# Tiles 4 to 7 as two units of two tiles instead of one of four, in a conditioned residual layer

## The chip, the cores and the metric

The kernel runs on one core of one Trainium2 chip. The metric is the device time of one execution in microseconds (us). Engines are called by the names that the profile uses: PE is the matrix engine (PEld its weight loads), DVE the vector engine, ACT the scalar engine, POOL the GpSimd engine, and SP the engine whose queue issues nearly all DMA transfers of this kernel.

## What is computed

```python
def _L0_cond_ref(hidden0, hidden1, x, W, b):     # x: (4, 1024, 512), W: (1536, 512)
    hidden = jnp.concatenate([hidden0, hidden1], axis=-1)         # both are cond_512: (4, 256)
    x_mean = jnp.mean(x, axis=1, keepdims=True)
    ones_L = jnp.ones((1, L, 1), dtype=x.dtype)
    fused = jnp.concatenate([x, x_mean * ones_L, hidden[:, None, :] * ones_L], axis=-1)
    return jax.nn.relu(jnp.einsum('bld,do->blo', fused, W) + b)
return x + _L0_cond_ref(cond_512, cond_512, x, L0_cond_W, L0_cond_b)
```

Each of the four batch rows has 1024 positions of 512 channels. Only the first third of W meets every position. The other two thirds meet the mean and the condition, which are the same for all positions of a row: they give one bias vector for each row.

## The kernel before

**Tiles and products.** The 4096 positions are 32 tiles of 128, eight to a batch row. A tile's product with the first third of W needs the tile transposed, with its 512 channels cut into J = 4 quarters of 128 (index j). Each float32 factor is split into a high and a low part (`w_hi`, `w_lo`; `his`, `los`), and each quarter takes three matmuls: hi by hi, lo by hi, hi by lo. `p5.2` is the triple of tile 5, quarter 2 (line 365); `p5.2.1` is one matmul of it. The 12 matmuls of a tile gather in one of five PSUM banks, `bank(t)` = `ps_o[t % 5]`.

**Units.** Tiles are transposed unit by unit (`UNITS`). Tiles 0 to 3 are units of one tile, transposed on PE from the plain copy of x. The others are units of four tiles. For these, four DMA transfers (`Zu.i`, 256 KB each) bring the tiles into one of three buffers `zs`, arranged so that DVE's transpose of 32x32 blocks finishes the job: `Tu.j` (line 258) transposes quarter j of all tiles of the unit, 128x512 elements, and needs all four transfers. `hu.j` (ACT, line 265) rounds it to `his` and adds up its columns into `sums`; `lu.j` (DVE or POOL, line 271) takes the remainder to `los`. Quarters 0 and 2 are turned into PSUM (`ps_x`), 1 and 3 into SBUF (`turned`): four slots, each of which is written again when the h and the l of its last content are done.

**Bias of a row.** When all sums of row r are in, `to` (POOL, lines 301 to 307) gives the mean. `as` (ACT, line 311) puts the condition's part (`ac`, `g`, `d`) into the bank `acc`; four `m` (DVE, line 316) add the mean times the second third of W, which the transfers `M0` to `M3` bring. Then `f` (ACT, line 324), `fa` (DVE, 328), `vh` (ACT, 332) and `vl` (DVE, 336) fold and split it, and `pb` (PE, line 340) spreads it over the partitions, from where `bc` (ACT) copies it to `biases`.

**The way out.** `K` (lines 436 and 438, from tile 12 on 446) empties a bank into a parking buffer, `b` and `r` add bias and apply relu, `F` adds x, and `S` stores the tile. F needs the plain copy of x, which `Xg.h` brings two tiles at a time.

**What sets the order.** Each engine runs its instructions in the order in which the names stand in `ORDER`, a list written out by hand or by a search; a letter behind @ names the engine where there is a choice (d DVE, a ACT, p POOL). An engine whose next instruction waits does nothing else. SP's transfers also go in this order, and at most eight are under way: each waits until the one eight before it has landed. PE's instructions around `pb0` stand in lines 33 and 34 of `ORDER`: eight triples of tiles 8 to 11, then `pb0`.

Of the kernel before, what the change touches and what calls it, by code (L numbers as in the profile page):

```python
# [25 lines left out]
h1.3 p1.0.1 Z4.1 p1.1.0 wh2@a l1.2@d p1.1.1 y2.0@d p0.2.0 wl2@p l1.3@d T2.0 T2.1 T2.2 T2.3 p1.2.0 Z4.3 p0.2.1 h2.0  # L26
h2.1 h2.2 h2.3 l2.0@d l2.1@d wh3@a C p1.2.1 p0.1.2 p1.1.2 l2.2@d l2.3@d wl3@d p2.0.0 p2.0.1 p0.2.2 V p0.3.0 B p1.3.0
y3.0@d p0.3.1 p1.3.1 T3.0 T3.1 T3.2 T3.3 p1.2.2 p0.3.2 h3.0 h3.1 p1.3.2 l3.0@d h3.2 l3.1@d p2.0.2 h3.3 l3.2@d l3.3@d
p2.1 p2.2 p2.3 p3.0 p3.1 Z5.0 Z5.2 Z5.1 p3.2 Z5.3 M1 M0 M2 Z6.0 M3 Z6.2 Z6.1 Z6.3 T4.0 T4.3 h4.0 T4.1 h4.3 l4.0@d h4.1
l4.3@p t3 p3.3 T4.2 Z7.0 Z7.2 Z7.1 Z7.3 K2@d l4.1@p K1@a p4.0 t2 h4.2 ac0@p p6.0 l4.2@d K0@a p4.3 t0 K3@d p5.3 t1  # L30
ac1@d g0.0 p7.2 p6.2 d0.0 g0.1 p5.2 d0.1 g1.0 p5.0 T5.1 T5.3 p5.1 d1.0 T5.2 p6.3 K5@a T5.0 Z8.0 Z8.2 X1.0 Z8.1 Z8.3
X1.1 as0 p4.2 to0 g1.1 p7.3 h5.1 m0.0 p6.1 g2.0 l5.1@p m0.1 p4.1 h5.2 m0.2 p7.1 K4@a m0.3 h5.3 p7.0 K6@a p8.1 l5.3@p
l5.2@d h5.0 p10.1 f0 d1.1 p9.1 fa0 p10.3 l5.0@d vh0 d2.0 p8.2 g2.1 vl0 p11.2 K7@a T6.3 d2.1 p11.3 T6.2 h6.3 p8.0 T6.0
# [1 line left out]
l6.2@d p12.3 r2@a m1.0 K9@a p8.3 F1@p S1 Z9.1 X3.0 Z9.3 T7.3 p11.0 T7.1 h7.3 p12.2 b0@p m1.1 h7.1 p12.0 T7.2 K8@a
p12.1 b3@p g3.0 T7.0 p11.1 K10@a m1.2 h7.2 d3.0 p13.1 m1.3 h7.0 p14.0 l7.0@d f1 b4@p p13.3 r0@a l7.2@d p14.1 r3@a T8.2
l7.3@p p15.0 fa1 p13.0 T8.0 vh1 F2@p S2 Z10.0 X2.1 Z10.2 p15.1 K11@a vl1 p13.2 F0@d S0 Z10.1 b6@p p15.2 T8.3 pb1
l7.1@p p14.3 bc1@a as2 p14.2 K13 F3@p r6@a p16.0 K12 h8.3 p15.3 K14 h8.2 l8.3@p T8.1 p17.0 b5@d h8.1 p19.3 b9@p h8.0
p17.3 r4@a l8.0@d p19.2 to2 g3.1 l8.2@d F4@p S4 Z10.3 X3.1 S3 p16.2 r5@a m2.0 p18.3 K15 b8@p p18.2 m2.1 p16.3 d3.1
m2.2 p19.0 m2.3 p18.1 F5@p S5 X5.0 T9.0 p16.1 f2 fa2 p20.3 b11@p T9.3 p17.2 vh2 h9.0 vl2 p17.1 F6@p S6 X4.0 X4.1 h9.3  # L40
T9.2 p19.1 l8.1@d b7@p p20.0 pb2 p18.0 bc2@a l9.3@p h9.2 p20.2 K17 r7@a p20.1 K16 as3 F7@p S7 X7.0 X6.1 X5.1 p22.2
T9.1 l9.0@d p21.3 h9.1 T10.0 r8@a p21.1 l9.1@p K19 r11@a p22.1 r9@a l9.2@d b10@p p22.0 r14@a K18 p21.2 r13@a T10.1
h10.0 p24.2 F13@p S13 T10.2 h10.1 p24.1 T10.3 h10.2 F8@p F9@d S9 S8 X6.0 p21.0 r15@a p24.0 r10@a F11@p S11 X7.1 K20
h10.3 p22.3 K21 r17@a p23.1 to3 r21@a p23.0 F10@p S10 m3.0 r18@a p23.3 r20@a m3.1 p26.1 l10.3@p m3.2 p25.0 K22 F21@p
S21 p23.2 m3.3 r22@a p26.2 F15@p S15 f3 p24.3 r12@a fa3 p27.3 F17@p S17 K23 vh3 p25.1 r16@a vl3 p25.2 r19@a F16@p S16
r23@a p26.0 l10.0@d p25.3 F19@p S19 pb3 p26.3 bc3@a F12@p S12 P28 p27.1 K25 p27.2 l10.2@d P30 F18@p p28.2 F14@d S14
S18 r25@a p30.2 l10.1@p K26 p28.0 F25@d S25 P31l p27.0 F23@p S23 r26@a p30.0 K24 p31.2l F26@p K27 p31.0l r24@a P29
p31.3l F20@p p30.3 p31.1l P31r F31l S31l S26 F22@d S22 S20 p29.1 p28.1 r27@d p29.0 F24@d S24 F27@p p28.3 p29.3 F28 S28
S27 p30.1 p29.2 F30 S30 p31.1r F29 S29 p31.0r p31.3r p31.2r F31r S31r
# [445 lines left out]
```

## Time and profile before

| | |
|---|---|
| time, median of 3 runs (lowest, highest) | 100.74 us (100.49, 102.19) |
| the profiled execution's own time | 101.55 us |
| its span, first to last instruction of the program | 99.8 us |
| busy in the span: PE, PEld | 95.2 us (95%), 76.3 us (76%) |
| busy in the span: POOL, DVE, ACT | 79.9 us (80%), 76.5 us (77%), 61.8 us (62%) |
| granted TensorE clock | 9 of 10 or more in all 40 slices of the span |

How to read it: the span leaves out 1.75 us that lie around the program in that execution. A busy share is an average over stages; whether an engine is waited for is told by the rows of that stage. Matmuls are pipelined, so the distance between two starts tells the pace, not the length of one row.

### The profile page before, as it was taken

To read this page: it belongs to the slowest core of one execution; us is meant where nothing else is said; L and a number is where in the kernel's file an instruction comes from. 1 tells how busy PE (TensorE), PEld (TensorE's weight loads), DVE (VectorE), ACT (ScalarE), POOL (GpSimd) and SP (SyncE) were. 2 spreads that over 40 slices of the span, in tenths; PEclk is the share of its full clock that TensorE was granted. 3 is DMA by queue.
4 is the path that set the end of the run, shared out by engine and by line. 5 is a ranking of instruction groups with operands and counts; after the bars stand their busy time and mean duration, and the time that the engine had idled before them with its cause. 6 is when DMAs were issued, how large, how long until landed. Compare 5 with 4: busy or idle time off the path is not lost.

```text
span 99.8 us, 1456 instructions
## 1 busy us (share of the span) xinstructions
PE 95.2 (95%) x426; PEld 76.3 (76%) x426; DVE 76.5 (77%) x131; ACT 61.8 (62%) x160; POOL 79.9 (80%) x77
## 2 busy tenths in 40 slices
...
GB/s 62 336 339 290 230 282 284 208 249 262 228 214 221 220 224 214 183 219 250 278 258 285 243 289 274 329 393 407 352 292 388 407 385 283 315 225 214 306 382 150
DMA packets 25361, 27.36 MB, mean 274 GB/s; under 512 B 1413, under 2 KB 16009, under 8 KB 25354
## 3 DMA queue, kind: packets, MB, share of 16 engines
...
q8 instruction: 3, 0.05, 0.2%
...
HBM read 18.88 MB, written 8.39 MB: 273 GB/s over the span
## 4 chain that ended last, share of the span: by engine, by line
PE 47%; DMA 35%; DVE 6%; SPq 6%; issue 1%; ACT 1%; DVEq 0%
PE po L365 46%; DMA x<-in_L_cond_W_dram 14%; DMA z<-in_x_dram 11%; DMA w_mean<-in_L_cond_W_dram 10%; SPq L145 6%; DVE lo L271 2%; DVE acc L328 1%; PE acc L340 1%; DVE acc L316 1%; DVE v_acc L336 1%; DVE o L236 1%; ACT fold L324 1%; ACT v_acc L332 1%; DVE w_hi L217 1%; DVE x L409 0%
## 5 line engine op out<-in xcount | busy, mean ns | idle before, releaser
L365 PE MATMUL po<-w_hi,hi 128*128 128x512 f32 (+1 forms) x133 | 50.6, 384 | 0.0
L365 PE MATMUL po<-w_hi,lo 128*128 128x512 f32 (+1 forms) x132 | 50.4, 384 | 0.0
L365 PE MATMUL po<-w_lo,hi 128*128 128x512 f32 (+1 forms) x132 | 50.1, 384 | 0.0
L460 POOL TENSOR_TENSOR x<-o,x 128x512 f32<-128x512 f32 x22 | 29.8, 1380 | 0.4 <-DVE o L451 0.4
L365 PEld LDWEIGHTS po<-w_hi,hi 128*128 128x128 f32 x133 | 24.9, 188 | 5.4 <-ACT o L438 0.6
L365 PEld LDWEIGHTS po<-w_hi,lo 128*128 128x128 f32 x132 | 24.8, 188 | 5.3 <-DVE lo L271 0.6
L365 PEld LDWEIGHTS po<-w_lo,hi 128*128 128x128 f32 x132 | 24.7, 188 | 4.9 <-POOL w_lo L221 0.2
L271 POOL TENSOR_TENSOR lo<-xT,hi 128x512 fp32r<-128x512 f32 x13 | 17.7, 1365 | 9.5 <-ACT hi L265 9.5
L453 ACT ACTIVATE o<-o 128x512 f32<-128x512 f32 x27 | 15.7, 621 | 3.3 <-DVE o L446 3.0
L442 POOL TENSOR_TENSOR o<-o,bias 128x512 f32<-128x512 f32 x10 | 13.8, 1390 | 0.0
L316 DVE SCALAR_TENSOR_TENSOR acc<-w_mean,tot,acc 128x512 f32<-128x512 f32 x16 | 12.0, 748 | 1.6 <-POOL tot L307 1.2
L265 ACT ACTIVATE hi<-px 128x512 fp32r<-128x512 f32 (+1 forms) x22 | 10.4, 477 | 4.1 <-DVE px L258 3.5
L446 DVE TENSOR_TENSOR o<-po,bias 128x512 f32<-128x512 f32 x16 | 10.5, 680 | 2.8 <-ACT bias L344 1.4
L258 DVE STREAM_TRANSPOSE px<-z 128x512 f32<-128x512 f32 x14 | 9.5, 699 | 3.7 <-DMA z<-in_x_dram 3.6
L271 DVE TENSOR_TENSOR lo<-px,hi 128x512 fp32r<-128x512 f32 (+1 forms) x22 | 11.6, 536 | 0.8 <-ACT hi L265 0.7
L258 DVE STREAM_TRANSPOSE xT<-z 128x512 f32<-128x512 f32 x14 | 9.4, 686 | 2.1 <-DMA z<-in_x_dram 2.1
L265 ACT ACTIVATE hi<-xT 128x512 fp32r<-128x512 f32 x14 | 8.8, 625 | 1.3 <-DVE xT L258 1.3
L293 ACT ACTIVATE term<-wc,cT 128x512 f32<-128x512 f32 x8 | 5.7, 716 | 2.3 <-DVE cT L279 1.6
L297 POOL TENSOR_TENSOR cond<-b_sb,term 128x512 f32<-128x512 f32 x4 | 5.2, 1300 | 1.0 <-ACT term L293 1.0
L438 ACT ACTIVATE o<-po 128x512 f32<-128x512 f32 x10 | 5.9, 586 | 0.1
L460 DVE TENSOR_TENSOR x<-o,x 128x512 f32<-128x512 f32 x6 | 5.6, 935 | 0.0
L297 POOL TENSOR_TENSOR cond<-cond,term 128x512 f32<-128x512 f32 x4 | 5.2, 1293 | 0.3 <-ACT term L293 0.2
...
## 6 DMA issues: line engine op xcount, KB each, us to landing
...
x<-in_L_cond_W_dram SPq DMA_DIRECT2D x1, 1024.0 KB, 10.0
...
```

The source lines that it names most:

```text
L145: (nc.scalar if e == "a" else nc.sync).dma_start(**kw)
L258: nc.vector.transpose(xT.rearrange("p (n q e) -> p n q e", q=Q // E, e=E), zs[z_of(u)][:, : n * NQ].rearrange("p n (q j e) -> p n j q e", ...
L265: nc.scalar.activation(his[buf][:, col : col + m], xT, AF.Copy, accum_out=sums[:, r, j, s : s + 1])
L271: nc_of[e].tensor_tensor(los[buf][:, col : col + m], xT, his[buf][:, col : col + m].bitcast(F32), ALU.subtract)
L297: nc.gpsimd.tensor_tensor(conds[r % 2], conds[r % 2] if k else b_sb, terms[k], ALU.add)
L316: nc.vector.scalar_tensor_tensor(acc, w_mean[:, j, :], tot[:, r, j : j + 1], acc, ALU.mult, ALU.add)
L365: nc.tensor.matmul(v, lhsT=a[:, col : col + P], rhs=m, start=WAYS[t] != "I" and key not in done, stop=done.count(key) == 3 * J - 1, skip_g ...
L438: nc.scalar.activation(o, bank(t), AF.Copy)
L442: nc_of[e].tensor_tensor(o, o, biases[r], ALU.add)
L446: nc.vector.tensor_tensor(o, bank(t), biases[r], ALU.add)
L453: nc.scalar.activation(o, o, AF.Relu)
L460: nc_of[e].tensor_tensor(x_tile(t), o, x_tile(t), ALU.add)
```

## The change

Tiles 4 to 7 become two units, (4, 2) and (6, 2). Unit 4 is tiles 4 and 5, unit 5 is tiles 6 and 7, and the later units are counted up by one: tiles 8 to 11 are unit 6 now, tiles 12 to 15 unit 7, and so on. Each of the two new units has its own four transfers of 128 KB into a half of the same buffer, and its own four T, h and l of 128x256 elements; so there are four transfers, T, h and l more. Row 0 has six units instead of five, and `to0` adds them in the same number of steps. The matmuls are the same ones. The middle of `ORDER` (the work between the first triples of tile 2 and `S1`) is written anew; behind it the old order goes on with the new unit numbers.

```diff
-l6.3@p T6.1 Z9.0 X2.0 Z9.2 pb0 p10.0 bc0@a h6.0 p10.2 b1@p h6.1 l6.0@d p9.3 h6.2 b2@d p9.0 as1 to1 p9.2 r1@a l6.1@p
...
+l6.2@d Z9.1 T7.3 d1.1 Z9.3 T7.1 T7.0 X1.0 p10.1 g2.1 d2.1 p9.3 T7.2 Z10.0 X2.0 Z10.2 p10.0 pb0 bc0@a b1@p h7.3 h7.1
...
-    UNITS = [(0, 1), (1, 1), (2, 1), (3, 1)] + [(t, 4) for t in range(4, NT, 4)]
+    UNITS = [(0, 1), (1, 1), (2, 1), (3, 1), (4, 2), (6, 2)] + [(t, 4) for t in range(8, NT, 4)]
...
-    sums = sb("sums", [P, B, J, 5])
+    sums = sb("sums", [P, B, J, 6])
     tot = sb("tot", [P, B, J])
-    pre = sb("pre", [P, J, 2])
+    pre = sb("pre", [P, J, 3])
...
     def z_of(u):
-        return (u - len(BY_PE)) % Z_BUFS
+        t0, n = UNITS[u]
+        return zs[(t0 // 4 - 1) % Z_BUFS][:, t0 % 4 * NQ : (t0 % 4 + n) * NQ]
...
-                dma(e, out=z[i * Q : (i + 1) * Q, : n * NQ], in_=zv[r, i, :, k0 * NQ : (k0 + n) * NQ, :])
+                dma(e, out=z[i * Q : (i + 1) * Q], in_=zv[r, i, :, k0 * NQ : (k0 + n) * NQ, :])
...
-                xT = (turned if j % 2 else ps_x)[j // 2]
+                xT = (turned if j % 2 else ps_x)[j // 2][:, :m]
...
-            if n == 5:
-                add(pre, v[:, :, :2], v[:, :, 2:4], ALU.add)
-                add(pre[:, :, 0], pre[:, :, 0], v[:, :, 4], ALU.add)
+            if n == 6:
+                add(pre, v[:, :, :3], v[:, :, 3:6], ALU.add)
+                add(pre[:, :, 0], pre[:, :, 0], pre[:, :, 2], ALU.add)
```

On PE, `pb0` now stands behind six triples of tiles 8 to 11 instead of eight. Three other places follow row by row.

**First place: DVE, tiles 4 to 7.** z_69 is the buffer of these tiles, px and xT the slots of a turned quarter, hi_78 belongs to tile 3, cT to the condition, o_105 and o_106 are banks being emptied (K2, K3). Before, from the first transpose of these tiles:

```order
L258 STREAM_TRANSPOSE px_140<-z_69 128x512
L258 STREAM_TRANSPOSE xT_121<-z_69 128x512
L258 STREAM_TRANSPOSE xT_120<-z_69 128x512
L271 TENSOR_TENSOR lo_93<-px_140,hi_79 128x512
L279 STREAM_TRANSPOSE cT<-bias_118 32x64
L258 STREAM_TRANSPOSE px_141<-z_69 128x512
L436 COPY o_105<-po_137 128x512
```

And now, from the same place; the first two transposes need the transfers of tiles 4 and 5 alone, the third those of tiles 6 and 7:

```order
L260 STREAM_TRANSPOSE xT_120<-z_69 128x256
L260 STREAM_TRANSPOSE xT_121<-z_69 128x256
L273 TENSOR_TENSOR lo_92<-acc,hi_78 128x128
L273 TENSOR_TENSOR lo_92<-po_139,hi_78 128x128
L273 TENSOR_TENSOR lo_92<-px_140,hi_78 128x128
L260 STREAM_TRANSPOSE xT_120<-z_69 128x256
L273 TENSOR_TENSOR lo_95<-xT_120,hi_81 128x256
L260 STREAM_TRANSPOSE px_140<-z_69 128x256
```

Two half transposes have moved ahead of tile 3's remainders, and a third ahead of tile 3's last remainder.

**Second place: DVE, from the transposes of tiles 8 to 11 to the end of row 0's bias.** z_70 is the buffer of these tiles, acc<-w_mean,tot,acc the four m0. Before:

```order
L258 STREAM_TRANSPOSE xT_120<-z_70 128x512
L258 STREAM_TRANSPOSE xT_121<-z_70 128x512
L258 STREAM_TRANSPOSE px_141<-z_70 128x512
L258 STREAM_TRANSPOSE px_140<-z_70 128x512
L316 SCALAR_TENSOR_TENSOR acc<-w_mean,tot,acc 128x512 x4
L271 TENSOR_TENSOR lo_99<-px_141,hi_85 128x512
L328 TENSOR_TENSOR acc<-acc,fold 64x512
L271 TENSOR_TENSOR lo_97<-px_140,hi_83 128x512
L336 TENSOR_TENSOR v_acc<-acc,v_acc 64x512
```

And now:

```order
L260 STREAM_TRANSPOSE xT_120<-z_70 128x512
L260 STREAM_TRANSPOSE xT_121<-z_70 128x512
L260 STREAM_TRANSPOSE px_141<-z_70 128x512
L319 SCALAR_TENSOR_TENSOR acc<-w_mean,tot,acc 128x512
L260 STREAM_TRANSPOSE px_140<-z_70 128x512
L439 COPY o_106<-po_138 128x512
L319 SCALAR_TENSOR_TENSOR acc<-w_mean,tot,acc 128x512 x3
L273 TENSOR_TENSOR lo_97<-px_140,hi_83 128x512
L331 TENSOR_TENSOR acc<-acc,fold 64x512
L339 TENSOR_TENSOR v_acc<-acc,v_acc 64x512
```

The first m0 stands before the last transpose, a bank's copy (K3) has come into the chain between the m0, and one remainder (l6.2) now stands behind v_acc.

**Third place: SP's transfers.** z_69 is here the buffer of tiles 16 to 19, z_70 of tiles 20 to 23, z_71 of tiles 24 to 27; x_66 is the plain copy of tiles 4 to 7. Before:

```order
L145 DMA z_69<-in_x_dram 32x16x128 x4
L145 DMA z_70<-in_x_dram 32x16x128 x2
L145 DMA x_66<-in_x_dram 128x2x512
L145 DMA z_70<-in_x_dram 32x16x128 x2
L145 DMA x_66<-in_x_dram 128x2x512
L145 DMA z_71<-in_x_dram 32x16x128
```

And now:

```order
L146 DMA z_69<-in_x_dram 32x16x128 x4
L146 DMA z_70<-in_x_dram 32x16x128 x4
L146 DMA x_66<-in_x_dram 128x2x512
L146 DMA z_71<-in_x_dram 32x16x128
L146 DMA x_67<-in_x_dram 128x2x512
```

The first half of x_66 has moved behind the last two transfers of tiles 20 to 23; its second half goes eight rows further back, behind the transfers of tiles 24 to 27. Further ahead, the four w_mean transfers now stand together; before, the fourth stood behind the first transfer of tiles 12 to 15.

## Rows read from the trace of the kernel before

**Rows 1.** The profile's page: the span and each engine's busy time.

```profile
span 99.8 us, 1456 instructions
PE 95.2 (95%) x426; PEld 76.3 (76%) x426; DVE 76.5 (77%) x131; ACT 61.8 (62%) x160; POOL 79.9 (80%) x77
```

**Rows 2.** The chain of waits in order of time: start us, us, what.

```profile
20.38 9.48 DMA w_mean<-in_L_cond_W_dram
...
35.61 10.99 DMA z<-in_x_dram
...
48.78 0.70 DVE v_acc L336
...
50.02 13.62 PE po L365 x60
```

**Rows 3.** The timeline of PE at 18 us: start us, us, engine line operation out<-in.

```profile
17.71 0.39 PE L365 MATMUL po<-w_hi,hi 128*128 128x512 f32 x1
18.11 0.50 PE L365 MATMUL po<-w_hi,lo 128*128 128x512 f32 x1
...
18.80 0.50 PE L365 MATMUL po<-w_hi,hi 128*128 128x512 f32 x1
19.13 0.40 PE L365 MATMUL po<-w_hi,lo 128*128 128x512 f32 x1
```

**Rows 4.** The timeline of DVE, tiles 4 to 7; in brackets idle time before, and releaser.

```profile
15.58 0.73 DVE L258 STREAM_TRANSPOSE px<-z 128x512 f32<-128x512 f32 x1 [2.23 <-DMA z<-in_x_dram]
...
17.41 0.65 DVE L271 TENSOR_TENSOR lo<-px,hi 128x512 fp32r<-128x512 f32 x1
```

**Rows 5.** The timeline of ACT, the copy of bank 1 (K1).

```profile
18.16 0.58 ACT L438 ACTIVATE o<-po 128x512 f32<-128x512 f32 x1
```

**Rows 6.** The timeline of PE at 49 us, the second row's bias (L340).

```profile
48.89 0.39 PE L365 MATMUL po<-w_lo,hi 128*128 128x512 f32 x1
49.52 0.50 PE L340 MATMUL acc<-v_acc,ones 128*128 128x512 f32 x1 [0.24 <-DVE v_acc L336]
49.86 0.39 PE L365 MATMUL po<-w_hi,hi 128*128 128x512 f32 x1
```

**Rows 7.** The timeline of PE, the first row's bias (pb0).

```profile
34.61 0.39 PE L340 MATMUL acc<-v_acc,ones 128*128 128x512 f32 x1
```

**Rows 8.** The timeline of DVE, tiles 8 to 11 and the first row's bias.

```profile
24.42 1.31 DVE L258 STREAM_TRANSPOSE xT<-z 128x512 f32<-128x512 f32 x2 [2.10 <-DMA z<-in_x_dram]
25.65 1.28 DVE L258 STREAM_TRANSPOSE px<-z 128x512 f32<-128x512 f32 x2
27.49 3.22 DVE L316 SCALAR_TENSOR_TENSOR acc<-w_mean,tot,acc 128x512 f32<-128x512 f32 x4 [0.56 <-POOL tot L307]
...
32.73 0.68 DVE L336 TENSOR_TENSOR v_acc<-acc,v_acc 64x512 fp32r<-64x512 f32 x1
```

**Rows 9.** The timeline of POOL, the same stretch.

```profile
25.12 1.30 POOL L297 TENSOR_TENSOR cond<-b_sb,term 128x512 f32<-128x512 f32 x1
...
27.23 0.22 POOL L307 TENSOR_SCALAR tot<-tot 128x4 f32<-128x4 f32 x1
...
29.41 1.29 POOL L271 TENSOR_TENSOR lo<-xT,hi 128x512 fp32r<-128x512 f32 x1 [0.70 <-ACT hi L265]
```

**Rows 10.** Groups by line and shape: line engine op shapes xcount | busy us, mean ns | idle.

```profile
L271 DVE TENSOR_TENSOR lo<-px,hi 128x128 fp32r<-128x128 f32 x8 | 2.2, 284 | 0.0
...
L436 DVE COPY o<-po 128x512 f32<-128x512 f32 x2 | 1.3, 667 | 0.0
...
L409 DVE SCALAR_TENSOR_TENSOR x<-po,x 128x256 f32<-128x256 f32 x2 | 0.8, 424 | 2.3 <-PE po L365 2.3
```

**Rows 11.** Stretches: us, busy us (instructions) of PE, PEld, DVE, ACT, POOL; PEclk, DMA share, GB/s.

```profile
40.00:45.00 5.00, 5.00 (x23) 4.14 (x23) 4.69 (x8) 4.96 (x13) 5.00 (x5) 1.00 1.15 201
...
65.00:70.00 5.00, 5.00 (x24) 4.14 (x23) 4.90 (x9) 4.65 (x11) 5.00 (x5) 1.00 1.04 400
```

**Rows 12.** The timeline of POOL, the residual add of tile 4 (F4).

```profile
56.10 1.29 POOL L460 TENSOR_TENSOR x<-o,x 128x512 f32<-128x512 f32 x1
```

More of the change, by code (lines that the diff above doesn't have):

```diff
@@ L25 @@
 T1.0 T1.1 T1.2 T1.3 wh1@d h1.0 p0.0.2 l1.0@d h1.1 p0.1.0 p1.0.0 Z4.2 h1.2 p0.1.1 l0.2@d l0.3@d wl1@p p1.0.2 l1.1@d
[L26 to L33, printed above, removed]
-l6.3@p T6.1 Z9.0 X2.0 Z9.2 pb0 p10.0 bc0@a h6.0 p10.2 b1@p h6.1 l6.0@d p9.3 h6.2 b2@d p9.0 as1 to1 p9.2 r1@a l6.1@p
@@ L35 @@
[L35 to L49, printed above, removed]
+h1.3 p1.0.1 Z4.1 p1.1.0 wh2@a l1.2@d p1.1.1 y2.0@d p0.2.0 wl2@p l1.3@d T2.0 T2.1 T2.2 T2.3 p1.2.0 Z4.3 Z5.0 Z5.2 Z5.1
@@ new lines @@
+Z5.3 p0.2.1 h2.0 h2.1 h2.2 h2.3 l2.0@d l2.1@d wh3@a C p1.2.1 p0.1.2 p1.1.2 l2.2@d p2.2 l2.3@d wl3@d p2.0.0 p2.0.1
+p0.2.2 V p0.3.0 B p1.3.0 y3.0@d p0.3.1 p1.3.1 T3.0 T3.1 T4.1 T3.2 T3.3 p1.2.2 p0.3.2 h3.0 p2.1 h3.1 K0@a T4.3 p1.3.2
+l3.0@d p3.0 h3.2 l3.1@d p3.1 l3.2@d h4.1 l4.1@p p5.1 T5.1 h5.1 l5.1@d T4.0 h4.3 Z6.3 l4.3@p p4.1 t3 t2 p3.2 p2.0.2
+h3.3 l3.3@d t1 t0 T4.2 p5.3 p3.3 ac0@p Z6.1 K1@a h4.0 Z6.0 p2.3 h4.2 T5.3 l4.2@d T5.2 p4.2 ac1@d p4.3 g0.0 l4.0@d p4.0
+T5.0 g0.1 h5.2 K2@d p5.2 h5.0 l5.2@d p6.2 d0.0 d0.1 h5.3 l5.3@p to0 p5.0 Z6.2 as0 M0 l5.0@d T6.1 g1.0 d1.0 p6.1 K4@a
@@ new lines @@
+T6.3 g1.1 M1 T6.2 h6.1 K5@a p6.0 l6.1@p p6.3 K6@a p7.2 g2.0 M3 h6.3 p7.1 m0.0 T6.0 h6.0 K3@d p7.3 p7.0 l6.3@p p9.1
+m0.1 M2 m0.2 m0.3 Z7.2 K7@a Z7.3 Z7.0 Z7.1 f0 l6.0@d fa0 h6.2 vh0 p8.1 p10.3 Z8.0 Z8.3 Z8.2 vl0 Z8.1 Z9.0 Z9.2 d2.0
+l6.2@d Z9.1 T7.3 d1.1 Z9.3 T7.1 T7.0 X1.0 p10.1 g2.1 d2.1 p9.3 T7.2 Z10.0 X2.0 Z10.2 p10.0 pb0 bc0@a b1@p h7.3 h7.1
+h7.0 p11.3 p10.2 l7.0@d h7.2 b2@d p9.0 l7.3@p as1 to1 p9.2 r1@a l7.1@p l7.2@d p8.0 p11.2 p12.3 p8.2 r2@a m1.0 K9@a
+p8.3 F1@p S1 Z10.1 X3.0 Z10.3 T8.3 p11.0 T8.1 h8.3 p12.2 b0@p m1.1 h8.1 p12.0 T8.2 K8@a p12.1 b3@p g3.0 T8.0 p11.1
@@ new lines @@
+K10@a m1.2 X1.1 h8.2 d3.0 p13.1 m1.3 h8.0 p14.0 l8.0@d f1 b4@p p13.3 r0@a l8.2@d p14.1 r3@a T9.2 l8.3@p p15.0 fa1
+p13.0 T9.0 vh1 F2@p S2 Z11.0 X2.1 Z11.2 p15.1 K11@a vl1 p13.2 F0@d S0 Z11.1 b6@p p15.2 T9.3 pb1 l8.1@p p14.3 bc1@a as2
+p14.2 K13 F3@p r6@a p16.0 K12 h9.3 p15.3 K14 h9.2 l9.3@p T9.1 p17.0 b5@d h9.1 p19.3 b9@p h9.0 p17.3 r4@a l9.0@d p19.2
+to2 g3.1 l9.2@d F4@p S4 Z11.3 X3.1 S3 p16.2 r5@a m2.0 p18.3 K15 b8@p p18.2 m2.1 p16.3 d3.1 m2.2 p19.0 m2.3 p18.1 F5@p
+S5 X5.0 T10.0 p16.1 f2 fa2 p20.3 b11@p T10.3 p17.2 vh2 h10.0 vl2 p17.1 F6@p S6 X4.0 X4.1 h10.3 T10.2 p19.1 l9.1@d b7@p
@@ new lines @@
+p20.0 pb2 p18.0 bc2@a l10.3@p h10.2 p20.2 K17 r7@a p20.1 K16 as3 F7@p S7 X7.0 X6.1 X5.1 p22.2 T10.1 l10.0@d p21.3
+h10.1 T11.0 r8@a p21.1 l10.1@p K19 r11@a p22.1 r9@a l10.2@d b10@p p22.0 r14@a K18 p21.2 r13@a T11.1 h11.0 p24.2 F13@p
+S13 T11.2 h11.1 p24.1 T11.3 h11.2 F8@p F9@d S9 S8 X6.0 p21.0 r15@a p24.0 r10@a F11@p S11 X7.1 K20 h11.3 p22.3 K21
+r17@a p23.1 to3 r21@a p23.0 F10@p S10 m3.0 r18@a p23.3 r20@a m3.1 p26.1 l11.3@p m3.2 p25.0 K22 F21@p S21 p23.2 m3.3
+r22@a p26.2 F15@p S15 f3 p24.3 r12@a fa3 p27.3 F17@p S17 K23 vh3 p25.1 r16@a vl3 p25.2 r19@a F16@p S16 r23@a p26.0
@@ L50 @@
+l11.0@d p25.3 F19@p S19 pb3 p26.3 bc3@a F12@p S12 P28 p27.1 K25 p27.2 l11.2@d P30 F18@p p28.2 F14@d S14 S18 r25@a
+p30.2 l11.1@p K26 p28.0 F25@d S25 P31l p27.0 F23@p S23 r26@a p30.0 K24 p31.2l F26@p K27 p31.0l r24@a P29 p31.3l F20@p
+p30.3 p31.1l P31r F31l S31l S26 F22@d S22 S20 p29.1 p28.1 r27@d p29.0 F24@d S24 F27@p p28.3 p29.3 F28 S28 S27 p30.1
+p29.2 F30 S30 p31.1r F29 S29 p31.0r p31.3r p31.2r F31r S31r
 """.split()
@@ L171 @@
             continue
-        z = zs[z_of(u)]
+        z = z_of(u)
         for i in range(NQ):
@@ L259, in _ @@
                     xT.rearrange("p (n q e) -> p n q e", q=Q // E, e=E),
-                    zs[z_of(u)][:, : n * NQ].rearrange("p n (q j e) -> p n j q e", j=J, e=E)[:, :, j],
+                    z_of(u).rearrange("p n (q j e) -> p n j q e", j=J, e=E)[:, :, j],
                 )
```

5 lines of the change are left out of this document (3 added, 2 removed).

## The prediction

> **What bounds the kernel now.** First the page's busy shares: PE 95.2 us of a span of 99.8 us, and PEld, its weight loads, 76 % [rows 1]. That alone does not say that PE is the limit of every stage, so the chain of waits comes next. Its last part is PE nearly alone: from 50.02 us it counts 60 matmuls in 13.62 us [rows 2], 0.227 us each. This is the pace at which PE goes when nothing keeps it waiting. What the kernel can win without taking matmuls away is what PE loses against this pace.
>
> The timeline of PE, read by the distance between starts, shows two places after the start-up. **At 18 us**: from 17.71 to 19.13 us there are four steps, 1.42 us instead of 0.91, so 0.51 us are lost [rows 3]. The two late ones wait for tiles 4 to 7. `p4.0.1` starts at 18.11, when DVE has finished l4.0 (17.41 + 0.65), and DVE had begun with these tiles at 15.58, after 2.23 us of idling for their transfers [rows 4]. `p6.0` at 18.80 waits for ACT's copy of bank 1, which ends at 18.74 [rows 5] and stood on ACT behind three h of this unit. **At 49 us**: from 48.89 to 49.86 there are two steps, 0.97 us instead of 0.45, so 0.52 us are lost; the matmul that spreads row 1's bias (`pb1`) waits for vl1 [rows 6]. The chain says why: a z transfer of tiles 20 to 23, issued at 35.61, landed 10.99 us later, at 46.60, and DVE's next transpose, ahead of fa1 and vl1 in its order, waited for it [rows 2]. The first row's `pb0`, at 34.61, had no wait, as vl0 ended 1.2 us before (32.73 + 0.68) [rows 7, 8].
>
> So 0.51 + 0.52 = 1.03 us are to be had, one per cent. That is less than the 2 % that a measurement of this kernel can tell from no change.
>
> **The change part by part.** *Matmuls:* none is added or removed, so 0.227 us each stays.
>
> *Halves for tiles 4 to 7.* The first unit needs half the bytes, so its transposes can begin while DVE before idled 2.23 us [rows 4], and l4.1, `p5.1` and `p4.1` come long before `p5.3` and `p4.0`. K0 and K1 are copied earlier in ACT's order. I take the wait at 18 us as gone: **-0.51**. Four T, h and l more cost DVE, ACT and POOL their fixed parts. No row has a half transpose or a half l. The nearest are an operation of DVE on 128x256 with 424 ns, and l on 128x128 with 284 ns [rows 10] beside 0.65 us on 128x512 [rows 4]: a line through these two gives 0.41 us at 256. I take 0.42 us; the bounds are 0.33 us, half of a whole one, and 0.65 us, as much as a whole one. DVE then does 13 halves (eight T, five l) for 5.5 us where it did four T and two l in some 4.1 us, 1.4 us more. They lie beside its two idle stretches of 2.23 us [rows 4] and 2.10 us [rows 8], so the path pays nothing.
>
> *The transfers of 128 KB* carry the same bytes; the DMA share stays above 1 (1.15 at 40 to 45 us [rows 11]), so the last bytes of tiles 4 to 7 and of tiles 8 to 11 should land when they did. What is late next, if tiles 6 and 7 come later than 15.5 us: the third transpose holds DVE, behind it l3.3, and by way of h5.1 and h4.3 on ACT also `p5.3`.
>
> *The mean chain of row 0.* Here something is moved onto the path. `pb0` stands two triples earlier, 6 x 0.227 = 1.36 us. With the first wait gone PE comes to it at 34.61 - 0.51 - 1.36 = 32.74 us. What has to be ready then is vl0. In the trace DVE gets tiles 8 to 11 at 24.42, transposes for 2.51 us to 26.93, idles 0.56 us for the mean, does four m0 in 3.22 us up to 30.71, and vl0 ends 2.70 us after that, at 33.41 [rows 8]. In the new order the idle 0.56 us should go: POOL now does `to0` ahead of the add that began at 25.12 before, so the mean that ended at 27.45 comes some 1.3 us earlier [rows 9]. But the copy of bank 3 has come into the chain, 0.67 us [rows 10]. 24.42 + 2.51 + 0.67 + 3.22 is 30.8; back-to-back operations of DVE overlap by some 0.08 us (two T take 1.31 and the next starts 1.23 after them [rows 8]), at three seams 0.2 us: 30.6 us. The rest of the chain stays 2.70 us: vl0 at 33.3 us. PE waits 33.3 - 32.74 = 0.56 us and pays another 0.11 us for the first step after a wait, as behind `pb1` (0.34 instead of 0.23) [rows 6]: **+0.67**. l6.3 on POOL would also be late for `p10.3` (the one at 29.41 ended at 30.70 [rows 9], PE wants it at about 30.2), but any wait of less than 0.56 us ahead of `pb0` is covered by the wait there.
>
> *The w_mean transfers together.* The fourth, which landed at 20.38 + 9.48 = 29.86 [rows 2], now has one transfer of 256 KB less ahead of it. At the 201 GB/s of the stretch in rows 11 that is 1.3 us: 28.6, and the third m0 wants it at about 28.9. No cost, with little to spare.
>
> *The plain copies of tiles 4 to 7 behind the z of tiles 20 to 23.* 512 KB at 201 GB/s are 2.6 us [rows 11], so the z that landed at 46.60 comes at about 44.0, before DVE has finished the two l that it did until 45.4. The wait at `pb1` goes: **-0.52**. The copies come later by as much; POOL's add of tile 4 does not start before 56.10 [rows 12].
>
> *Behind 50 us* the order is the old one. POOL is busy for all of 65 to 70 us and DVE for 4.90 of 5.00 [rows 11], so a PE that came much earlier would catch up with them; at some 0.4 us I cost that at nothing.
>
> **Sum:** -0.51 + 0.67 - 0.52 = -0.36 us. The span goes from 99.8 to 99.4 us, the profiled execution from 101.55 to 101.2. That execution was 0.81 us above the median of the runs, 100.74; the difference carried over, I predict 100.4 us.
>
> **The rivals.** *No wait at pb0* (0.22). If tiles 8 to 11 land 0.6 us earlier, or the seams on DVE overlap more, vl0 is ready in time. For it: the order puts the first m0 ahead of the last transpose. Against it: the transposes began at 24.42 because of a transfer, and nothing ahead of that transfer has fewer bytes. Then -1.03: 99.7 us.
>
> *Slower, by the mean chain* (0.20). The fourth w_mean transfer lands as late as before, 29.86, because the four together get no more bandwidth. The third m0 then waits 0.95 us, vl0 ends at 34.25 and `pb0` costs 0.95 more: 101.35 us. The point from which the change loses is a landing at 28.9 + 0.36 = 29.3 us. For it: the same queue, full all the time. Against it: the transfer of z that was ahead of it is now behind.
>
> *DVE becomes the bound between 15 and 25 us* (0.05). If a half costs as much as a whole, 0.65 us, DVE has 13 x 0.23 = 3.0 us more than I count. Of the idle 2.10 us before 24.42 [rows 8] some 1.2 us are left after the halves that I do count, so the transposes of tiles 8 to 11 and all behind them come 1.8 us later: 102.2 us. It begins to cost at halves of 0.51 us. Against it are the 424 ns of rows 10. [...]
>
> *The change does nothing* (0.05): the wait at 18 us only moves to `p6.2` or `p5.3`, the one at 49 us stays: 100.7 us.
>
> **How the numbers follow.** The forecast (0.48) has its own range of 100.0 to 100.8, by 0.4 us of the chain either way. The whole range, 99.5 to 101.5, takes in the first two rivals and leaves out the slow DVE and rare pile-ups. Faster by over 2 % would be below 98.7, which even both waits gone do not give: 0.02. Slower by over 2 % is above 102.8: half of the DVE case in a bad form and a chain that is late at both ends, 0.05. The rest, 0.93, is within 2 %.
>
> **What would show it.** Right: no step over 0.3 us on PE between 17 and 20 us; one of 0.6 to 1.0 us at the first L343 row, near 33 us, released by DVE v_acc; none at the second; PE at its 0.227 us from there on; half transposes near 0.4 us. Wrong: a wait on PE before 24 us put down to DVE's lo, a third m0 that waits for w_mean, or a transpose of tiles 20 to 23 that still idles for its transfer.

## The result, and the profile of the changed kernel

| | kernel before | changed kernel |
|---|---|---|
| time, median of 5 runs each (lowest, highest) | 100.74 us (100.49, 102.19) | 102.11 us (101.95, 102.32) |
| ratio to the kernel before, 95 % interval | | 1.0123 (1.0074 to 1.0173) |
| profiled execution: its own time, span | 101.55 us, 99.8 us | 101.95 us, 100.1 us |

The change made the kernel slower by about one per cent, which is still within 2 %. The forecast was 100.4 us with a range of 99.5 to 101.5 us; the time lies above that range.

The page of the changed kernel, the span and the busy times, to be read beside [rows 1]:

```profile
span 100.1 us, 1475 instructions
PE 94.7 (95%) x426; PEld 76.7 (77%) x426; DVE 78.4 (78%) x138; ACT 62.5 (62%) x168; POOL 79.3 (79%) x78
```

DVE is busy for 78.4 us instead of 76.5 us. The halves explain 1.3 us of that: the eight T and five l of 128x256 took 5.4 us (the rows of 128x256 further below), where four T and two l of twice the size took some 4.1. Another 0.97 us is in one other row (L289 below; rows overlap at their seams, by 0.08 us at the end of this one, so the two together come to more than the 1.9 us between the busy times). The chain of waits of the changed kernel shows where that row lies (start us, us, what):

```profile
20.07 0.46 DVE px L260
20.53 1.57 DVE wc L289
22.11 0.34 DVE lo L273
22.45 0.04 issue
22.49 11.70 PE po L368 x50
34.19 0.23 PE acc L343
34.42 15.64 PE po L368 x69
50.06 0.23 PE acc L343
50.29 13.60 PE po L368 x60
```

From 22.49 us to the end PE runs at its pace: 50 matmuls in 11.70 us, 69 in 15.64, 60 in 13.60, 0.227 to 0.234 us each, and each `pb` (L343) takes 0.23 us. Neither `pb` waits, where `pb1` waited in [rows 2, 6]. Behind the start-up, nearly all that is lost lies ahead of 22.49, behind one row: `ac1` (L289, the second sum of the condition's part of W), 1.57 us of the chain. PE's timeline at that place (columns as in [rows 3], in brackets idle time before, and releaser):

```profile
21.13 0.39 PE L368 MATMUL po<-w_lo,hi 128*128 128x512 f32 x1
21.36 0.39 PE L368 MATMUL po<-w_hi,hi 128*128 128x512 f32 x1
22.49 0.50 PE L368 MATMUL po<-w_hi,lo 128*128 128x512 f32 x1 [0.75 <-DVE lo L273]
22.83 0.40 PE L368 MATMUL po<-w_lo,hi 128*128 128x512 f32 x1
```

Two steps, from 21.36 to 22.83, take 1.47 us instead of 0.45: 1.02 us are lost at the second matmul of `p4.0`, which waits for l4.0 on DVE. DVE and POOL in the same stretch, from the timeline of all engines of the changed kernel:

```profile
20.07 0.46 DVE L260 STREAM_TRANSPOSE px<-z 128x256 f32<-128x256 f32 x1
...
20.27 1.29 POOL L299 TENSOR_TENSOR cond<-b_sb,term 128x512 f32<-128x512 f32 x1 [1.26 <-ACT term L295]
...
20.44 1.66 DVE L289 TENSOR_TENSOR wc<-x 128x512 f32<-128x512 f32 x1
...
22.03 0.41 DVE L273 TENSOR_TENSOR lo<-px,hi 128x256 fp32r<-128x256 f32 x1
```

POOL began `d0.0` (L299, the first addition to row 0's condition part) at 20.27 and was in it until 21.56. DVE began `ac1` 0.17 us later and needed 1.66 us, until 22.11, which is 0.55 us behind the end of POOL's instruction. l4.0 stands right behind `ac1` in DVE's order and so began at 22.03. In the kernel before, `ac1` met no instruction of POOL, and the same operation took 0.69 us. Groups by line and shape, first of the kernel before, then of the changed kernel (columns as in [rows 10]):

```profile
L460 DVE TENSOR_TENSOR x<-o,x 128x512 f32<-128x512 f32 x6 | 5.6, 935 | 0.0
...
L442 DVE TENSOR_TENSOR o<-o,bias 128x512 f32<-128x512 f32 x2 | 2.5, 1262 | 0.0
...
L271 DVE TENSOR_TENSOR lo<-xT,hi 128x512 fp32r<-128x512 f32 x1 | 1.1, 1085 | 0.0
...
L287 DVE TENSOR_TENSOR wc<-x 128x512 f32<-128x512 f32 x1 | 0.7, 691 | 0.0
```

```profile
L260 DVE STREAM_TRANSPOSE px<-z 128x256 f32<-128x256 f32 x4 | 1.8, 444 | 0.1
L289 DVE TENSOR_TENSOR wc<-x 128x512 f32<-128x512 f32 x1 | 1.7, 1664 | 0.0
L260 DVE STREAM_TRANSPOSE xT<-z 128x256 f32<-128x256 f32 x4 | 1.6, 421 | 2.2 <-DMA z<-in_x_dram 1.3 <-POOL lo L273 0.9
L273 DVE TENSOR_TENSOR lo<-px,hi 128x256 fp32r<-128x256 f32 x4 | 1.6, 411 | 0.2 <-ACT hi L267 0.2
...
L273 DVE TENSOR_TENSOR lo<-xT,hi 128x256 fp32r<-128x256 f32 x1 | 0.4, 427 | 0.6 <-ACT hi L267 0.6
```

The sign was there in the kernel before, and the prediction did not read it: additions and subtractions of DVE with both inputs in SBUF had means of 691, 935, 1085 and 1262 ns for one shape, while those with one input in PSUM (l from px: 679 ns) varied only from 651 to 692 ns. One of the slow ones beside its neighbour, from the timeline of the kernel before:

```profile
36.25 1.30 POOL L442 TENSOR_TENSOR o<-o,bias 128x512 f32<-128x512 f32 x1
...
36.85 1.25 DVE L442 TENSOR_TENSOR o<-o,bias 128x512 f32<-128x512 f32 x1
```

POOL's row ends at 37.55, DVE's at 38.10: 0.55 us later, as in the changed kernel. The duration follows from that: 0.69 us, and as much more as POOL's instruction still has to go when DVE begins, less 0.14 us (37.55 - 36.85 - 0.14 = 0.56 and 1.25 - 0.69 = 0.56; for `ac1` 21.56 - 20.44 - 0.14 = 0.98 and 1.66 - 0.69 = 0.97). It is no matter of two chosen rows: all eight additions and subtractions of DVE in the kernel before that have this shape and both inputs in SBUF, and began inside an instruction of POOL, ended 0.55 us behind it.

### The profile page after: what moved, and what is told of

It is laid out like the page before. It is cut to its first block, busy times and chain, and to the rows that moved or that the text cites. A ratio compares the mean times of both kernels' runs of the same rounds, so it can differ in the third digit from the quotient of the medians.

```text
span 100.1 us, 1475 instructions
## 1 busy us (share of the span) xinstructions
PE 94.7 (95%) x426; PEld 76.7 (77%) x426; DVE 78.4 (78%) x138; ACT 62.5 (62%) x168; POOL 79.3 (79%) x78
## 4 chain that ended last, share of the span: by engine, by line
PE 76%; DVE 6%; issue 6%; DMA 3%; ACT 3%; POOL 2%; POOLq 0%
PE po L368 74%; DMA x<-in_x_dram 3%; ACT hi L267 2%; DVE wc L289 2%; DVE lo L273 1%; POOL w_lo L223 1%; DVE px L260 1%; DVE cT L281 1%; PE acc L343 1%; POOL lo L273 1%; PE px L258 1%; ACT w_hi L217 1%; DVE xT L260 0%; PE po L258 0%; DVE x L412 0%
## 5 line engine op out<-in xcount | busy, mean ns | idle before, releaser
L273 POOL TENSOR_TENSOR lo<-xT,hi 128x512 fp32r<-128x512 f32 (+1 forms) x14 | 16.9, 1210 | 7.9 <-ACT hi L267 7.9
L445 POOL TENSOR_TENSOR o<-o,bias 128x512 f32<-128x512 f32 x10 | 14.3, 1431 | 0.0
L273 DVE TENSOR_TENSOR lo<-px,hi 128x512 fp32r<-128x512 f32 (+2 forms) x24 | 11.8, 505 | 1.4 <-ACT hi L267 1.2
L267 ACT ACTIVATE hi<-px 128x512 fp32r<-128x512 f32 (+2 forms) x24 | 10.7, 449 | 1.6 <-DVE px L260 1.1
L260 DVE STREAM_TRANSPOSE xT<-z 128x512 f32<-128x512 f32 (+1 forms) x16 | 9.8, 624 | 2.5 <-DMA z<-in_x_dram 1.3
L267 ACT ACTIVATE hi<-xT 128x512 fp32r<-128x512 f32 (+1 forms) x16 | 9.1, 571 | 2.4 <-DVE xT L260 2.3
L260 DVE STREAM_TRANSPOSE px<-z 128x512 f32<-128x512 f32 (+1 forms) x16 | 10.0, 637 | 0.1
L299 POOL TENSOR_TENSOR cond<-cond,term 128x512 f32<-128x512 f32 x4 | 5.2, 1295 | 2.3 <-DVE px L260 1.4
L299 POOL TENSOR_TENSOR cond<-b_sb,term 128x512 f32<-128x512 f32 x4 | 5.2, 1298 | 1.3 <-ACT term L295 1.3
L463 DVE TENSOR_TENSOR x<-o,x 128x512 f32<-128x512 f32 x6 | 6.1, 1014 | 0.0
```

The source lines that it names most:

```text
L260: nc.vector.transpose(xT.rearrange("p (n q e) -> p n q e", q=Q // E, e=E), z_of(u).rearrange("p n (q j e) -> p n j q e", j=J, e=E)[:, :, j],)
L267: nc.scalar.activation(his[buf][:, col : col + m], xT, AF.Copy, accum_out=sums[:, r, j, s : s + 1])
L273: nc_of[e].tensor_tensor(los[buf][:, col : col + m], xT, his[buf][:, col : col + m].bitcast(F32), ALU.subtract)
L299: nc.gpsimd.tensor_tensor(conds[r % 2], conds[r % 2] if k else b_sb, terms[k], ALU.add)
L445: nc_of[e].tensor_tensor(o, o, biases[r], ALU.add)
L463: nc_of[e].tensor_tensor(x_tile(t), o, x_tile(t), ALU.add)
```

## The experiments

The theory after this result: `ac1` meets `d0.0`, waits until POOL's instruction ends, and holds l4.0. The rivals: the execution profiled was unlucky; the half-size work on DVE is what is late; the transfers are.

### The kernel before once more (e1_before_again)

No edit.

> The kernel before, unchanged, for a second profile of it: five runs of it lay between 100.49 and 102.19 us, and the profiled one was among the slow ones at 101.55. If the run is near 100.7, its span is near 99.0 us, and one of the two waits of PE (0.51 us at 18 us, 0.52 us at 49 us) is gone or smaller in it. If they stand as before, the 0.8 us between the runs lie elsewhere.

Its time was 101.5 us, somewhat above the median of 29 executions of the kernel before that were measured with it (median 101.26 us, 100.48 to 102.86). In its trace neither of the two waits of [rows 3] and [rows 6] stands: PE runs through 18 us, and `pb1` goes at 48.56 us without a wait. In their place PE loses 1.09 us near 69.6 us, at a tile of the last row:

```profile
68.74 0.39 PE L365 MATMUL po<-w_lo,hi 128*128 128x512 f32 x1
69.58 0.50 PE L365 MATMUL po<-w_hi,hi 128*128 128x512 f32 x1 [0.45 <-DVE o L446]
70.18 0.50 PE L365 MATMUL po<-w_hi,lo 128*128 128x512 f32 x1
70.51 0.39 PE L365 MATMUL po<-w_lo,hi 128*128 128x512 f32 x1
```

DVE had idled 1.74 us there, up to a transpose at 68.23, and the last of the z transfers for it landed at 68.05; that it waited for this transfer is read from the two times, since the profile names no releaser there. So the waits of the kernel before hang on late transfers and move from one execution to the next. This bears on two terms of the prediction, below.

### `ac1` one place earlier on DVE (e2_ac1_one_earlier)

```diff
-... T5.3 l4.2@d T5.2 p4.2 ac1@d p4.3 g0.0 l4.0@d p4.0
+... T5.3 l4.2@d ac1@d T5.2 p4.2 p4.3 g0.0 l4.0@d p4.0
```

> The changed kernel with two neighbours on DVE exchanged: ac1 runs ahead of T5.2 instead of behind it. The work of every engine is the same. Theory (DVE's ac1 reads and writes SBUF alone, and has to wait until the instruction that POOL is in, d0.0, is over): ac1 now begins near 20.0 us, when POOL is idle, and takes 0.69 us instead of 1.66; the step of 1.14 us on PE at p4.0 falls under 0.35 us, the transposes of tiles 8 to 11 begin about 1 us earlier; 0.8 to 1.1 us less than the changed kernel's 102.1: 101.0 to 101.3. Rival (DVE has too much work there, 13 halves for 6 whole ones): the order of two neighbours changes nothing, PE still waits about 1 us in all for DVE between 20 and 24 us, 101.9 to 102.3.

Median 100.82 us (12 runs, all but one within 100.65 to 101.07), ratio to the kernel before 0.9963 (0.9935 to 0.9991). DVE and POOL, from the timeline of all engines:

```profile
19.90 0.68 DVE L289 TENSOR_TENSOR wc<-x 128x512 f32<-128x512 f32 x1
...
20.21 1.53 POOL L299 TENSOR_TENSOR cond<-b_sb,term 128x512 f32<-128x512 f32 x1 [1.26 <-ACT term L295]
20.50 0.45 DVE L260 STREAM_TRANSPOSE px<-z 128x256 f32<-128x256 f32 x1
...
20.86 0.40 DVE L273 TENSOR_TENSOR lo<-px,hi 128x256 fp32r<-128x256 f32 x1
```

`ac1` now begins 0.31 us ahead of `d0.0` and takes 0.68 us; this time POOL's instruction is the longer one, 1.53 instead of 1.29 us. l4.0 begins at 20.86, 1.17 us earlier. PE has no step above 0.34 us from 12 us to the end. Moving one name in DVE's order by one place makes it 1.29 us less than the 102.11 us of the changed kernel (1.11 us less than the 101.93 us of its second measurement, below). That is a little more than the 0.8 to 1.1 us expected. This version is faster than the changed kernel by about one per cent, and than the kernel before by 0.4 %.

### `ac1` on POOL (e3_ac1_on_pool)

```diff
-... T5.2 p4.2 ac1@d p4.3 g0.0 l4.0@d p4.0
+... T5.2 p4.2 ac1@p p4.3 g0.0 l4.0@d p4.0
```

> The changed kernel with ac1 on POOL (1.29 us there) instead of DVE. Theory: POOL does ac0 and ac1 back to back from 17.7 to 20.3 us, d0.0 is not later than before, DVE is free of 1.66 us; no wait on PE at p4.0, none at pb0, vl0 ends before 32.5 us; 1.0 to 1.2 us less than the changed kernel: 100.9 to 101.1. Rival (too much work on DVE): the same direction, but only by the 0.69 us that ac1 would cost alone, 101.4.

Median 100.88 us (100.74 to 101.66), ratio 0.9986 (0.9955 to 1.0018). Taken off DVE altogether, `ac1` can meet nothing there, and the time is that of the version above within 0.1 us, at the lower end of what was expected. So it was not DVE's 0.69 us for `ac1` that cost, but the meeting.

### `d0.0` in four parts (e4_d0_in_quarters)

```diff
-                nc.gpsimd.tensor_tensor(conds[r % 2], conds[r % 2] if k else b_sb, terms[k], ALU.add)
+                n = 4 if (r, k) == (0, 0) else 1
+                for i in range(n):
+                    c = slice(i * D // n, (i + 1) * D // n)
+                    src = conds[r % 2] if k else b_sb
+                    nc.gpsimd.tensor_tensor(conds[r % 2][:, c], src[:, c], terms[k][:, c], ALU.add)
```

> The changed kernel with d0.0 on POOL cut into four instructions of 128 columns; ac1 stays where it is. Theory, with the wait lasting until the end of POOL's instruction in progress: ac1 gets through after the first or second quarter, takes 0.7 to 1.1 us instead of 1.66, and the step at p4.0 shrinks from 1.14 us to 0.3 to 0.6; 0.5 to 0.8 us less than the changed kernel: 101.3 to 101.6. If DVE has to wait for POOL to be idle altogether, ac1 takes 1.9 us or more and the time is 102.2 or more. Rival (too much work on DVE): 102.1, and ac1 as long as before.

Median 101.47 us (101.3 to 101.75), ratio 1.0034 (1.0006 to 1.0063). POOL was as busy beside `ac1` as in the changed kernel, but in instructions of a quarter of the length. The time is within the forecast, and so is the step on PE at `p4.0`, 0.34 us. The timeline of DVE, and of POOL, of this kernel:

```profile
20.29 0.84 DVE L289 TENSOR_TENSOR wc<-x 128x512 f32<-128x512 f32 x1
21.05 0.41 DVE L273 TENSOR_TENSOR lo<-px,hi 128x256 fp32r<-128x256 f32 x1
```

```profile
20.12 2.17 POOL L303 TENSOR_TENSOR cond<-b_sb,term 128x128 f32<-128x128 f32 x4 [1.22 <-ACT term L295]
```

With nothing but the length of POOL's instructions changed, `ac1` fell from 1.66 to 0.84 us, at the same place in the order. DVE waited for the one instruction that POOL was in, not for POOL to be idle: `ac1` ended at 21.13 us, POOL's four at 22.29. Of the 1.29 us between the medians of the changed kernel and the version above 0.64 came back (0.46 of 1.11 us by the changed kernel's second measurement). 0.15 us of the rest is that `ac1` is still longer than 0.69. Another 0.19 us is lost on PE near 75 us, far from `ac1`: the chain has 81 matmuls in 18.55 us there, and 18.36 us in the version above. Where the remainder is was not followed up.

### The changed kernel once more (e8_after_again)

No edit.

> The changed kernel once more, in the same comparison as the three others. Theory: the collision of ac1 on DVE with d0.0 on POOL is set by the order and not by a late transfer, so it is in every execution: ac1 takes 1.5 to 1.8 us again, l4.0 ends near 22.4 us, and the times lie within 0.3 us of 102.1. Rival: it was chance in the first profile; then ac1 takes 0.7 us and the time is near 101 us.

Median 101.93 us (101.74 to 102.31, 6 runs), ratio 1.0076 (1.0046 to 1.0106) against 23 executions of the kernel before, whose median was 100.99 us. One of the six times, 101.74 us, lies 0.36 us from 102.1, where at most 0.3 us was expected. At this place the trace repeats the first one to 0.01 us, with a step of 1.14 us on PE (timeline of all engines):

```profile
20.27 1.29 POOL L299 TENSOR_TENSOR cond<-b_sb,term 128x512 f32<-128x512 f32 x1 [1.25 <-ACT term L295]
...
20.44 1.66 DVE L289 TENSOR_TENSOR wc<-x 128x512 f32<-128x512 f32 x1
...
22.02 0.41 DVE L273 TENSOR_TENSOR lo<-px,hi 128x256 fp32r<-128x256 f32 x1
```

The meeting belongs to the order and is in each of the two executions that were profiled; it was no accident of the first.

### The split alone (e5_split_alone, e9_split_alone_mended)

The kernel before with only the names of tiles 4 to 7 doubled, each half behind the other, and the rest of the order as it was, but for K0, which stands a few places earlier:

```diff
-... T4.0 T4.3 h4.0 T4.1 h4.3 l4.0@d h4.1 l4.3@p t3 p3.3 T4.2 ... K2@d l4.1@p K1@a ... l4.2@d K0@a ...
+... T4.0 T4.3 h4.0 T4.1 h4.3 l4.0@d T5.0 h5.0 l5.0@d h4.1 l4.3@p T5.3 h5.3 l5.3@p t3 p3.3 T4.2 ...
+... K2@d l4.1@p K1@a K0@a T5.1 h5.1 l5.1@p ... l4.2@d T5.2 h5.2 l5.2@d ...
```

> The kernel before with only the split: tiles 4 to 7 become two units of two (transfers, T, h and l half as large), each half behind the other in the old order; the plain copies X1.0 and X1.1, pb0 and the w_mean transfers stay where they were. Theory: the transfers come earlier because of the split itself (in the changed kernel the last z of tiles 6 and 7 landed at 14.24 us instead of 15.46, that of tiles 8 to 11 at 21.96 instead of 24.20). Then they land here within 0.5 us of 14.24 and 21.96, the wait for l4.0 near 18 us is gone, and the time is 100.5 to 101.1 us, if ac1 on DVE meets no instruction of POOL (if it does, up to 1 us more, to be seen as an ac1 of over 1 us). Rival: it is the new order that brings them earlier (C issued sooner, w_mean together); then tiles 8 to 11 land here at 23 to 24.2 us as in the kernel before, and the time is that of before, 101.0 to 101.6 us.

In this first version the transfers of tiles 16 to 19, which write the same buffer, stood ahead of `T5.1` and `T5.2`, so that these two transposed tiles 16 to 19 in place of 6 and 7 and waited for them: DVE was idle for 16.73 us, up to 34.44. Its time, 120.02 us, says nothing of the split, and only its first 17 us, and the landing of transfers issued in them, are read here. The other run has these transfers behind `T5.2`:

> The kernel before with only the split, as the run e5_split_alone, in which the transfers of tiles 16 to 19 stood ahead of the last two transposes of tiles 6 and 7 whose buffer they write; here these transfers stand behind them. Theory: the split alone brings the transfers earlier (in e5_split_alone, whose start is the same up to 17 us, the last z of tiles 6 and 7 landed at 14.08 us and that of tiles 8 to 11 at 21.64). Then tiles 8 to 11 land near 21.6 us, the wait for l4.0 near 18 us is gone, and the time is 100.5 to 101.1 us, up to 1 us more if DVE's ac1 meets an instruction of POOL (to be seen as an ac1 of over 1 us). Rival: DVE now has eight half transposes and five half l in the order of before, one behind the other, and PE waits for tiles 4 to 7 between 18 and 22 us; then a step of over 0.4 us on PE stands there and the time is 101.3 to 102.3 us.

Median 102.92 us (102.73 to 103.27), ratio 1.0192 (1.0145 to 1.0239): slower than the changed kernel too, above the 100.5 to 101.1 us of the theory and even above the 101.3 to 102.3 us of the rival. The transfers did come as the theory had it: the last z of tiles 8 to 11 landed at 21.91 us. `ac1` met nothing (0.69 us). But the rival's wait stands on PE at 21.47 us:

```profile
20.20 0.39 PE L366 MATMUL po<-w_lo,hi 128*128 128x512 f32 x1
21.47 0.50 PE L366 MATMUL po<-w_hi,hi 128*128 128x512 f32 x1 [0.88 <-ACT hi L265]
21.93 0.50 PE L366 MATMUL po<-w_hi,lo 128*128 128x512 f32 x1
22.27 0.40 PE L366 MATMUL po<-w_lo,hi 128*128 128x512 f32 x1
```

and DVE's timeline of this kernel shows what made it late:

```profile
18.60 0.45 DVE L258 STREAM_TRANSPOSE xT<-z 128x256 f32<-128x256 f32 x1 [0.76 <-POOL lo L271]
...
19.99 0.42 DVE L271 TENSOR_TENSOR lo<-px,hi 128x256 fp32r<-128x256 f32 x1 [0.67 <-ACT hi L265]
20.45 0.46 DVE L258 STREAM_TRANSPOSE px<-z 128x256 f32<-128x256 f32 x1
21.45 0.43 DVE L271 TENSOR_TENSOR lo<-px,hi 128x256 fp32r<-128x256 f32 x1 [0.54 <-ACT hi L265]
```

In this order the second unit's transposes wait for the first unit's l to free the slot that both use, and DVE idles between ACT and POOL: 0.76, 0.67 and 0.54 us. PE loses 1.39 us to it in three steps, and some 0.7 us more between 65 and 77 us, which was not followed up. So the split with this order is no gain. The changed kernel's order makes room for it, and with `ac1` out of the way the whole change is worth 0.4 % (0.1 to 0.65 %), or 0.2 % (0.0 to 0.4 %) with the plain copies of tiles 4 to 7 in their old place (next section).

### The plain copies of tiles 4 to 7 (e6_x_old_place, e7_before_x_late)

Two kernels. In the one, the version with `ac1` earlier gets X1.0 and X1.1 back to their old places:

```diff
-l6.2@d Z9.1 T7.3 d1.1 Z9.3 T7.1 T7.0 X1.0 ...      -K10@a m1.2 X1.1 h8.2 ...
+l6.2@d X1.0 Z9.1 T7.3 d1.1 Z9.3 X1.1 T7.1 T7.0 ...  +K10@a m1.2 h8.2 ...
```

> The changed kernel with ac1 one place earlier on DVE (the version of 100.82 us) and with the plain copies of tiles 4 to 7, X1.0 and X1.1, put back ahead of the last z transfers of tiles 20 to 23. The prediction's theory: this 512 KB is what the z of tiles 20 to 23 waited for. Then it lands at about 43.5 to 44 us instead of 41.07, and since DVE comes to those tiles only near 45 us, no more than 0.3 us is lost at pb1: 100.8 to 101.1 us in this profile, but with a wider spread of the times than 100.65 to 101.07, because late landings come through again. Rival: the wait had nothing to do with X1.0; the landing stays at 41 to 42 us and the times at 100.8 with the same narrow spread.

Median 100.83 us (100.64 to 101.06, 12 runs), ratio 0.9979 (0.9956 to 1.0002). The last z of tiles 20 to 23 landed at 44.50 us, where it landed at 40.94 us with the copies behind it: 3.6 us for 512 KB, so the copies do delay it. But DVE came to these tiles only at 44.63 us, so nothing waited, though by only 0.13 us, and the spread stayed narrow, which the theory had not expected.

In the other, the kernel before gets only this move (X1.0 behind `Z8.3`, X1.1 behind `Z9.3`):

> The kernel before with only X1.0 and X1.1 put later (behind the four z transfers of tiles 20 to 23, and behind those of tiles 24 to 27's first half), without the split. The prediction priced this at -0.52 us. Theory: the spread of the kernel before (100.48 to 102.86 us) comes from z transfers that land late behind these copies. Then the transposes of tiles 20 to 23 do not wait, the median is 100.5 to 100.9 us and most times lie within 0.4 us of it. Rival: the late landings come from elsewhere (the queue as a whole is full); the median stays at 101.0 to 101.5 us with the same spread, and a wait for a z shows at another place.

Median 100.92 us (all but one of 12 within 100.58 to 101.07, as narrow as expected), ratio 0.9978 (0.9954 to 1.0001). The last z of tiles 20 to 23 landed at 41.71 us instead of the 46.60 of [rows 2], and PE has no step above 0.32 us from 12 us on. The move alone, then, is worth 0.0 to 0.5 %, and about 0.07 us between the medians: its price in the prediction, 0.52 us, is paid only in executions in which that transfer is late.

## Why the prediction was wrong

**The step that failed is a term that the prediction put at nothing without a reason: the new place of `ac1` on DVE.** It prices DVE's work between 15 and 25 us by the halves alone ("They lie beside its two idle stretches of 2.23 us [rows 4] and 2.10 us [rows 8], so the path pays nothing") and has no term for what else the new order moves there. For the halves it was right: they took 0.41 to 0.44 us where 0.42 was taken, and in the two versions without the meeting, which have all thirteen of them, PE has no step above 0.34 us from 12 us on. The one l from xT of this size, both inputs in SBUF and POOL idle, took 427 ns. On ACT and POOL too a half took more than half as long as a whole: in the changed kernel h from px 375 ns against 590, l on POOL 738 to 741 ns against 1292 to 1310 (one, begun beside an addition of DVE, took 1744). What was not asked is which instructions DVE would have beside POOL's in the new order. `ac1`, moved 1.2 us earlier, came to begin 0.17 us behind `d0.0`. It cost 0.97 us more than its row, l4.0 behind it was on the path, and PE lost 1.02 us. The two versions without the meeting (100.82 and 100.88 us), the one with shorter POOL instructions (0.84 us for `ac1`) and the repetition show this, and not only argue it. The prediction had named the sign, "a wait on PE before 24 us put down to DVE's lo", but priced what would cause it, a DVE that is the bound, by slow halves alone.

The runs have the meeting in both directions: with `ac1` second, it took 1.66 instead of 0.69 us; with `d0.0` second, that took 1.53 instead of 1.29 us.

**-0.51 at 18 us.** The step on PE between 17 and 20 us is gone, as predicted. But the wait was that of one execution: it comes when the last z of tiles 4 to 7 lands at 15.46 us, as in the profile that was read, and not when it lands at 14.87 or 14.43 us, as in the two other traces of that order.

**-0.52 at 49 us.** Gone too, and the copies do delay the transfer, as the prediction had it (it landed at 40.94 us with them behind it, at 44.50 us with them ahead). But the move was not needed for the wait to go: with the copies in their old place `pb1` did not wait either, and in the repetition of the kernel before, where that transfer landed at 45.13 us, it did not. So this too was a wait of the one execution that was read.

**The sum's base.** Both terms were taken off an execution of 101.55 us, and then its 0.81 us above the median were taken off once more. But the waits are most of what sets that execution above others: 101.55 - 0.51 - 0.52 = 100.52 us, close to the fastest run of the kernel before in each measurement (100.37 to 100.49), and the repetition gives 101.50 - 1.09 = 100.41. With the waits counted once, the best that the change could give was about 100.5 us, and the version without the meeting has 100.82. The three terms do not close the sum of the two profiled executions: -0.51 - 0.52 + 1.02 is -0.01 us, measured was +0.40 us (101.95 against 101.55). 0.28 us of that lies ahead of the first triple, which PE began at 5.10 instead of 4.82 us; in the second traces of the two kernels it began at 4.96 and 4.88 us.

**+0.67 at `pb0`.** No wait came. vl0 ended at 33.44 us (33.3 predicted), but PE was at `pb0` only at 34.03, since it had lost 1 us before. In the version without the meeting vl0 ends at 32.32 and PE comes at 32.91, so there is no wait either. The chain from the first transpose of tiles 8 to 11 to the end of vl0 was put at 8.9 us and measured 9.4 us in both. What was wrong was its start: 24.42 us was taken, and it was 24.09 us in the changed kernel, where `ac1` had held DVE, and 22.91 us in the version without the meeting. Tiles 8 to 11 landed over 0.6 us earlier in both (21.96 and 21.91 us instead of 24.20), which is the condition of the first rival. In the changed kernel DVE came to them late all the same, and it was PE's own delay that left no wait: without it PE would have been there at 34.03 - 1.02 = 33.01 us, ahead of vl0.

**"The last bytes of tiles 4 to 7 and of tiles 8 to 11 should land when they did."** Wrong. The last z of tiles 8 to 11, first in the kernel before and then in the changed kernel (issued at 13.46 us, 0.02 us after the transfer eight places ahead of it had landed, and at 14.12 us; the last column is the time from issue to landing):

```profile
z<-in_x_dram SPq DMA_DIRECT2D x1, 256.0 KB, 10.7
```

```profile
z<-in_x_dram SPq DMA_DIRECT2D x1, 256.0 KB, 7.8
```

It landed at 24.20 and at 21.96 us. Part of that is again the one execution: in the other two traces of the old order of transfers it landed at 22.95 and 22.22 us. In the eight traces with the split it landed at 21.64 to 22.35 us. The last z of tiles 4 to 7 came at 15.46, 14.87 and 14.43 without the split, at 13.81 to 14.48 with it. The ranges touch, and there are only three traces without the split: that the split makes these transfers earlier is likely but not shown, and what in it would do so was not tested.

**The w_mean transfers** kept no `m` waiting, as forecast. **The rival "slower"** had the sign right and the place wrong: it was put into the mean chain, and none of its conditions came.
